# Layer 0's softmax division, taken apart into steps that lie in the next half head

## The chip, the cores and the metric

The kernel runs on one core of a Trainium2 chip. The metric is the device time of one execution in microseconds (us). Every time below comes from runs and from one profiled execution of the kernel before the change. The engines are named as the profile names them: PE (TensorE, with its weight loads as PEld), DVE (VectorE), ACT (ScalarE), POOL (GpSimd) and SP (SyncE, which here only issues transfers).

## The reference

Four images of 32 x 32 pixels and 384 channels go through four layers, each `x = x + layer(group_norm(x))`. All data are 32-bit floats.

```python
# layer 0: deformable attention, 6 heads of 64 channels, n = 1024 pixels
q = x @ w_q + b_q
offset = tanh(gelu(layer_norm(grouped_conv3x3(q))) @ w_offp) * 16
pos = offset + ref
xs = bilinear_sample(x, pos)                  # per group
k, v = xs @ w_k + b_k, xs @ w_v + b_v
attn = einsum('bmhc,bnhc->bhmn', q, k) * scale
bias = bilinear_sample(rpe, (ref - pos) / 2)  # 1024 x 1024 per head
attn = softmax(attn + bias, axis=-1)
out = einsum('bhmn,bnhc->bmhc', attn, v) @ w_out + b_out
# layer 1: attention of 12 heads of 32 channels, weighted by products of
#          sigmoid similarities, normalised over the queries
# layer 2: windowed sums of squares, num / denum
# layer 3: a 3 x 3 neighbourhood attention (softmax over 9), folded back
```

The change concerns the last step of layer 0's softmax: the division of `exp(...) @ v` by the sum of the exponentials.

## The kernel before, in words

Two generators write the program. `Front.layer0` is layer 0 of an image, `Trunk.image` is layers 1 to 3 of an image. Layer 0 of image 0 is written first, alone. Then the trunk of image b is written step by step, and after each step `Net.layer3` (the driver below) takes steps of layer 0 of image b + 1, as many as their yielded weights ask for. The trunk of the last image stands alone again. A scheduler then orders the instructions of each engine by dependence, priority and expected times; an instruction given to `keep_in_program_order` (`pin`) stays behind the one that was written before it on its engine. [...]

Layer 0's attention runs over six heads h and two halves q of 512 queries: twelve half heads an image, each one call of `head0(h, q)`. The keys j come in eight blocks of 128. For each j, POOL gathers a window of the position bias (`win`, L734), ACT and DVE interpolate it (`z`: L746, L747; `lg`: L751, L752), PE multiplies keys by queries (L755), DVE adds the product to the bias (L756) and keeps a running maximum (L759, L761). After the eighth block PE transposes the maxima (L768), DVE reduces them (`top`, L772), POOL makes a diagonal of them (L774), PE spreads it over the partitions (L776) and ACT copies it out (`tb`, L780). Then for each j DVE subtracts `tb` (L787), ACT takes the exponential (L788), and PE multiplies it by the values and by ones (L790), which gives the undivided output and the sums in one bank. ACT copies the output over the queries in `qpad` (L794) and the row of sums out (L797), and SP stores the row to `den` in DRAM (L798). Thirteen buffers hold the `lg` tiles: eight logits of the half head at work, the rest for the next one's bias, which the scheduler brings forward.

After two heads, `over_sums(k)` divides channel block k of `qpad` by the sums of heads 2k and 2k + 1. It loads the sums from DRAM with the pixels on the partitions (`dens`, two transfers, L807), takes the reciprocal (L808), stores it to `rden` (two transfers, L811), loads it back spread over 64 partitions per head into two `lg` tiles (four transfers, L816), and multiplies (two instructions, L821). After the third division, layer 0's output projection (L376, called from the loop at L427) reads `qpad`, DVE adds bias and residual (L432), and SP stores the result for the trunk.

In the trunk, layer 1 runs over six pairs of heads. The lines that matter here: Ln of the softmax sums (L1057) and the row of them stored and loaded again (L1063, L1011), four sigmoids of the similarities (L1081, after the matmuls L1074), logits (L1154) and their exponentials (L1162), the weights (L1184) and their product with the exponentials (L1193), and beside these the sums of the next pair (L1035, L1043, L1044). The other transfers of a pair are qa and ka (L1005), xg and gc (L1020, L1021), the values vp (L1102) and the result yd (L1215, from ACT's copy L1212). Exp, Sigmoid, Ln and Sqrt each make ACT load another table when they follow one another. Layer 2 ends with matmuls L1301, reciprocals L1323 and two more DVE steps (L1324, L1325), and statistics (L306, L307) for the norm of layer 3 (L330, L340), which needs its own weights `gmat`.

Of the kernel before, what the change touches and what calls it, by code (L numbers as in the profile page):

```python
# [21 lines left out]
ALU = mybir.AluOpType  # L22
# [4 lines left out]
P = 128  # L27
NB, HW, C = 4, 32, 384
N = HW * HW
KC = C // P  # L30
NJ = N // P
G, GC = 6, 64
# [32 lines left out]
def bc(ap, axis, n):  # L65

    u = ap.unsqueeze(axis)
    shape = list(u.shape)
    shape[axis] = n
    return u.broadcast_to(shape)  # L70


class Net:
# [183 lines left out]
    def layer0(self, b):  # L257

        if b == 0:
            for _ in self.front.layer0(b):  # L260
                pass
            self.done = self.ahead = 0.0
            self.fronts = (w for i in range(1, NB) for w in self.front.layer0(i))
# [135 lines left out]
class Front(Lane):  # L399


    def layer0(self, b):
        nc, v = self.nc, self.nc.vector
        with self.scope("l0"):
            self.qpad = self.wt([P, KC, PW, PW], "qpad")
            nc.gpsimd.memset(self.qpad, 0.0)

            self.kz = [self.wt([P, N], f"kz{r}") for r in range(2)]
            for r in range(2):
                nc.gpsimd.memset(self.kz[r][GC * (1 - r) : GC * (2 - r), :], 0.0)  # L410
            self.va = self.wt([P, NJ, C], "va")
            self.f = self.wt([P, 2, 2, NJ * G], "bias_f")
            self.widx = self.wt([P, 2, NJ * G], "widx", 1, I32)
            with self.scope("l0a"):
                yield from self.inputs0(b)
            with self.scope("l0b"):
                self.load_keys(0)
                for h in range(G):
                    if h + 1 < G:
                        self.load_keys(h + 1)  # L420
                    for q in range(2):
                        yield from self.head0(h, q)
                    if h % 2:
                        yield from self.over_sums(h // 2)
            with self.scope("l0c"):
                w = self.weights("w_out")
                for ko in range(KC):  # L427
                    rows = slice(ko * P, (ko + 1) * P)
                    x = self.wt([P, N], "res", 2)
                    nc.sync.dma_start(x, self.x0[b % 2][rows, :])  # L430
                    ps = self.dense_t(w, self.qpad, ko)
                    v.scalar_tensor_tensor(x, ps, self.col(C_BOUT, ko), x, ALU.add, ALU.add)  # L432
                    nc.sync.dma_start(self.x1[b % 2][rows, :], x)
                    yield 6
# [281 lines left out]
        rows = slice((h % 2) * GC, (h % 2 + 1) * GC)  # L716
        self.nc.sync.dma_start(self.kz[h % 2][rows, :], self.k0[h * GC : (h + 1) * GC, :])

    def head0(self, h, q):

        nc, v = self.nc, self.nc.vector
        f, kz, va = self.f, self.kz[h % 2], self.va
        k, r0 = h // 2, (h % 2) * GC
        rows = slice(r0, r0 + GC)
        other = slice(GC - r0, 2 * GC - r0)
        HH, HN = HW // 2, N // 2
        both = self.qpad[:, k, 1 + HH * q : 1 + HH * (q + 1), 1 : 1 + HW]
        queries = both[rows]
        logits = []
        rmax = self.wt([P, HN], "rmax", 2)  # L730
        for j in range(NJ):
            c = j * G + h
            win = self.wt([P, (HH + 1) * WROW], "win", 4)
            nc.gpsimd.indirect_dma_start(  # L734
                out=win,
                out_offset=None,
                in_=self.strips[:, :],
                in_offset=bass.IndirectOffsetOnAxis(
                    ap=self.widx[:, q, c : c + 1], axis=0
                ),  # L740
            )
            wv = win.rearrange("p (r c) -> p r c", c=WROW)
            sc = lambda i, t: f[:, i, t, c : c + 1]

            z = self.wt([P, HH, HW + 1], "z", 3)
            nc.scalar.activation(z, wv[:, 0:HH, 0 : HW + 1], AF.Copy, scale=sc(1, 1))  # L746
            v.scalar_tensor_tensor(  # L747
                z, wv[:, 1 : HH + 1, 0 : HW + 1], sc(0, 1), z, ALU.mult, ALU.add
            )
            lg = self.wt([P, HH, HW], "lg", 13)  # L750
            nc.scalar.activation(lg, z[:, :, 0:HW], AF.Copy, scale=sc(1, 0))  # L751
            v.scalar_tensor_tensor(lg, z[:, :, 1 : HW + 1], sc(0, 0), lg, ALU.mult, ALU.add)  # L752
            lf = lg.rearrange("p y x -> p (y x)")
            ps = self.bank()
            nc.tensor.matmul(ps, kz[:, j * P : (j + 1) * P], both, start=True, stop=True)  # L755
            v.tensor_tensor(lf, ps, lf, ALU.add)  # L756
            logits.append(lf)
            if j == 1:
                v.tensor_tensor(rmax, logits[0], lf, ALU.max)  # L759
            elif j > 1:  # L760
                v.tensor_tensor(rmax, rmax, lf, ALU.max)  # L761
            yield 3


        NI = HN // P
        ps = self.bank()
        for i in range(NI):
            nc.tensor.transpose(  # L768
                ps[:, i * P : (i + 1) * P], rmax[:, i * P : (i + 1) * P], self.ident
            )  # L770
        top = self.wt([P, NI], "top", 2)
        v.tensor_reduce(top, ps.rearrange("p (i n) -> p i n", i=NI), AX.X, ALU.max)  # L772
        diag = self.wt([P, NI, P], "diag", 1)
        nc.gpsimd.tensor_tensor(diag, bc(self.ident, 1, NI), bc(top, 2, P), ALU.mult)  # L774
        ps = self.bank()
        nc.tensor.matmul(  # L776
            ps, self.ones, diag.rearrange("p i n -> p (i n)"), start=True, stop=True
        )
        tb = self.wt([P, HN], "tb", 2)
        nc.scalar.copy(tb, ps)  # L780
        yield 3


        po = self.bank()
        for j in range(NJ):
            lf = logits[j]
            v.tensor_tensor(lf, lf, tb, ALU.subtract)  # L787
            nc.scalar.activation(lf, lf, AF.Exp)  # L788
            for out, w in ((rows, va[:, j, h * GC : (h + 1) * GC]), (other, self.ones[:, 0:GC])):
                nc.tensor.matmul(po[out, :], w, lf, start=j == 0, stop=j == NJ - 1)  # L790
            if j % 2:
                yield 2

        nc.scalar.copy(queries, po[rows, :].rearrange("p (y x) -> p y x", y=HH))  # L794
        o0 = other.start
        den = logits[0][o0 : o0 + 1, :]
        nc.scalar.copy(den, po[o0 : o0 + 1, :])  # L797
        nc.sync.dma_start(self.den[h][:, q * HN : (q + 1) * HN], den)  # L798
        yield 3

    def over_sums(self, k):

        nc, v = self.nc, self.nc.vector
        t = self.wt([P, 2, NJ], "dens", 2)
        for r in range(2):
            h = 2 * k + r
            nc.sync.dma_start(t[:, r, :], self.den[h].rearrange("o (p i) -> (o p) i", p=P))  # L807
        v.reciprocal(t, t)  # L808
        for r in range(2):
            h = 2 * k + r  # L810
            nc.sync.dma_start(self.rden[h].rearrange("o (p i) -> (o p) i", p=P), t[:, r, :])  # L811
        HH, HN = HW // 2, N // 2
        for q in range(2):
            inv = self.wt([P, HH, HW], "lg", 13)
            for r in range(2):
                nc.sync.dma_start(  # L816
                    inv[r * GC : (r + 1) * GC].rearrange("p y x -> p (y x)"),
                    self.rden[2 * k + r][0, q * HN : (q + 1) * HN].partition_broadcast(GC),
                )
            out = self.qpad[:, k, 1 + HH * q : 1 + HH * (q + 1), 1 : 1 + HW]  # L820
            v.tensor_tensor(out, out, inv, ALU.mult)  # L821
        yield 2


class Trunk(Lane):
# [717 lines left out]
```

## Time and profile before

| What | us |
|---|---|
| Median of 3 runs | 4879.74 |
| Lowest and highest of them | 4869.65, 4883.42 |
| The profiled execution | 4916.4 |
| Its span, first to last instruction | 4914.6 |

| Engine | busy us | share of the span |
|---|---|---|
| PE | 4251.9 | 87% |
| PEld | 1829.4 | 37% |
| DVE | 3177.4 | 65% |
| ACT | 2331.1 | 47% |
| POOL | 934.4 | 19% |

The shares are averages over stages with different limits. Layer 0 of image 0 takes about the first 650 us, and PE is busy in less than three quarters of most of it. Then PE is busy nine tenths of nearly every fortieth of the span, until layers 2 and 3 of the last image. The trunk of the last image starts near 4056 us. Stages are therefore read one by one, from windows of the trace. In the timeline lines of this document the first column is the start in us from the span's start and the second the length; in brackets stand the idle time of the engine ahead of the instruction and what ended it.

### The profile page before, as it was taken

The page shows a single profiled execution, that of the slowest core. Times are in us where ns is not written, and L with a number is a line of the kernel's source. Part 1 is how long each engine was busy: PE and PEld are TensorE (multiplying, and loading weights), DVE is VectorE, ACT ScalarE, POOL GpSimd, SP SyncE. Part 2 cuts the span into 40 slices and gives each one's busy share as a digit, 9 for nine tenths or more (in the row PEclk, how much of TensorE's full clock was granted, in tenths as well). Part 3 has the DMA queues.
Part 4 walks back from the last instruction along what each step waited for, and adds up shares of the span by engine and source line. Part 5 has one row for each costly group of instructions (what it writes and reads, how often), then busy time and mean ns, then how long its engine had stood idle before and what let it go on. Part 6 is the DMA issues. An engine that isn't in the chain of part 4 may idle for free.

```text
span 4914.6 us, 46753 instructions
## 1 busy us (share of the span) xinstructions
PE 4251.9 (87%) x15800; PEld 1829.4 (37%) x15800; DVE 3177.4 (65%) x5715; ACT 2331.1 (47%) x3623; POOL 934.4 (19%) x946
## 2 busy tenths in 40 slices
PE   5466677999999989889999989899999998999998
PEld 2222243333333453333333444343333335343444
DVE  3478827676878736577877763767687873455544
ACT  2155523565766213376666412356576721466630
POOL 1533203211212101331221110422121200000000
PEclk7677787999999989799999989799999998899998
DMA  5322244211212143331221123422121213201011
GB/s 116 106 81 87 69 128 143 92 55 38 76 47 74 33 145 111 104 95 49 66 58 58 55 75 111 151 88 58 32 78 44 78 34 111 91 24 30 18 38 39
DMA packets 230929, 366.84 MB, mean 75 GB/s; under 512 B 117476, under 2 KB 164673, under 8 KB 230689
## 3 DMA queue, kind: packets, MB, share of 16 engines
q1 hardware_dynamic: 169672, 197.36, 13.5%
q0 software_dynamic: 39936, 145.53, 9.7%
q10 hardware_dynamic: 21080, 20.96, 1.7%
q8 instruction: 125, 2.05, 0.2%
q14 instruction: 116, 0.94, 0.1%
HBM read 285.84 MB, written 78.21 MB: 74 GB/s over the span
## 4 chain that ended last, share of the span: by engine, by line
PE 50%; DVE 11%; ACT 11%; issue 5%; DMA 2%; POOL 1%; another core or an unknown queue 0%; SPq 0%; ACTq 0%; DVEq 0%; POOLq 0%
PE bank L1184 10%; PE big L376 5%; PE big L1154 5%; PE big L1035 4%; PE bank L755 4%; PE bank L790 4%; PE bank L390 3%; PE bank L1128 3%; ACT big L1044 3%; PE bank L1179 2%; PE big L1284 2%; DVE e L1193 2%; DVE nmax L1043 2%; ACT e L1162 1%; PE big L584 1%
## 5 line engine op out<-in xcount | busy, mean ns | idle before, releaser
L1193 DVE SCALAR_TENSOR_TENSOR e<-bank,gam,e 128x512 f32<-128x512 f32 x768 | 558.2, 749 | 568.3 <-ACT gn L1192 274.5
L1184 PE MATMUL bank<-sim,sg 128*128 128x512 f32 (+3 forms) x2304 | 879.6, 516 | 6.2 <-POOL sg L1139 3.7
L1044 ACT ACTIVATE big<-big,nmax 128x1024 f32<-128x1024 f32 x384 | 418.5, 1090 | 392.2 <-DVE nmax L1043 340.4
L734 POOL DMA_INDIRECT win<-strips,widx x384 | 421.2, 1097 | 876.6 <-DVE z L747 450.7
L1184 PEld LDWEIGHTS bank<-sim,sg 128*128 128x128 f32 x2304 | 408.7, 200 | 386.2 <-issue 303.6
L1162 ACT ACTIVATE e<-big 128x1024 f32<-128x1024 f32 x384 | 376.7, 1019 | 359.9 <-PE big L1154 354.7
L1043 DVE TENSOR_REDUCE nmax<-big 128x1 f32<-128x1024 f32 x384 | 453.7, 1219 | 74.4 <-PE big L1035 46.5
L1035 PE MATMUL big<-k,q 32*128 32x512 f32 x1536 | 353.6, 691 | 86.6 <-ACT e L1162 36.6
L1154 PE MATMUL big<-qa,ka 64*128 64x512 f32 x1536 | 412.9, 629 | 14.8 <-ACT big L1044 8.9
L1139 POOL TENSOR_SCALAR sg<-sim,gam 128x512 f32<-128x512 f32 x192 | 148.2, 774 | 1429.3 <-PE bank L1184 1135.5
L790 PE MATMUL bank<-lg,va 128*64 128x512 f32 x768 | 373.6, 635 | 39.8 <-ACT lg L788 39.7
L755 PE MATMUL bank<-qpad,kz 128*128 128x512 f32 x768 | 378.2, 622 | 21.4 <-DVE e L1193 13.2
L790 PE MATMUL bank<-lg,ones 128*64 128x512 f32 x768 | 372.9, 635 | 0.0
L746 ACT ACTIVATE z<-win,bias_f 128x528 f32<-128x528 f32 x384 | 277.2, 738 | 181.5 <-DVE lg L752 105.3
L752 DVE SCALAR_TENSOR_TENSOR lg<-z,bias_f,lg 128x512 f32<-128x512 f32 x384 | 300.8, 798 | 45.5 <-ACT lg L751 43.7
L747 DVE SCALAR_TENSOR_TENSOR z<-win,bias_f,z 128x528 f32<-128x528 f32 x384 | 292.0, 781 | 36.0 <-DMA win<-strips,widx 24.3
L652 POOL DMA_INDIRECT gat<-pairs,sidx x192 | 206.2, 1074 | 485.6 <-DVE ix_gt L464 241.6
L756 DVE TENSOR_TENSOR lg<-bank,lg 128x512 f32<-128x512 f32 x384 | 256.9, 685 | 60.3 <-PE bank L755 58.7
L787 DVE TENSOR_TENSOR lg<-lg,tb 128x512 f32<-128x512 f32 x384 | 250.6, 711 | 61.3 <-ACT tb L780 61.3
L751 ACT ACTIVATE lg<-z,bias_f 128x512 f32<-128x512 f32 x384 | 268.0, 719 | 44.3 <-DVE z L747 27.4
L788 ACT ACTIVATE lg<-lg 128x512 f32<-128x512 f32 x384 | 223.2, 630 | 85.4 <-DVE lg L787 85.1
L1154 PEld LDWEIGHTS big<-qa,ka 64*128 64x128 f32 x1536 | 135.8, 189 | 272.2 <-issue 157.0
(253 smaller groups left out, 5844.8 us busy)
## 6 DMA issues: line engine op xcount, KB each, us to landing
pairs<-xn SPq DMA_DIRECT2D x64, 192.0 KB
q<-qd SPq DMA_DIRECT2D x48, 256.0 KB
w<-in_gmat SPq DMA_DIRECT2D x16, 576.0 KB
w<-in_w_off SPq DMA_DIRECT2D x12, 576.0 KB
w<-in_Wqkv SPq DMA_DIRECT2D x12, 576.0 KB
a<-in_x SPq DMA_DIRECT2D x16, 384.0 KB
x<-a ACTq DMA_DIRECT2D x4, 1536.0 KB
k<-a SPq DMA_DIRECT2D x12, 512.0 KB
```

The source lines that it names most:

```text
L734: nc.gpsimd.indirect_dma_start(out=win, out_offset=None, in_=self.strips[:, :], in_offset=bass.IndirectOffsetOnAxis(ap=self.widx[:, q, c : ...
L747: v.scalar_tensor_tensor(z, wv[:, 1 : HH + 1, 0 : HW + 1], sc(0, 1), z, ALU.mult, ALU.add)
L752: v.scalar_tensor_tensor(lg, z[:, :, 1 : HW + 1], sc(0, 0), lg, ALU.mult, ALU.add)
L755: nc.tensor.matmul(ps, kz[:, j * P : (j + 1) * P], both, start=True, stop=True)
L790: nc.tensor.matmul(po[out, :], w, lf, start=j == 0, stop=j == NJ - 1)
L1035: nc.tensor.matmul(ps[r][:, h * 512 : (h + 1) * 512], self.q4[rows, i * P : (i + 1) * P], self.k4[rows, 0:512], start=True, stop=True,)
L1043: v.tensor_reduce(nmax[:, r, i : i + 1], ps[r], AX.X, ALU.max, negate=True)
L1044: nc.scalar.activation(ps[r], ps[r], AF.Exp, bias=nmax[:, r, i : i + 1], accum_out=den[:, r, i : i + 1],)
L1154: nc.tensor.matmul(ps[:, r, :], ka[rows, j * P : (j + 1) * P], qa[rows, cols], start=True, stop=True,)
L1162: nc.scalar.activation(e, ps, AF.Exp)
L1184: nc.tensor.matmul(ps[:, (mid - i0) * P :], sg[:, r, m, :], sim[:, r, m, mid * P : i1 * P], start=m == 0, stop=m == 1,)
L1193: v.scalar_tensor_tensor(e[:, r, :], ps, self.gam[:, 1:2], e[:, r, :], ALU.add, ALU.mult, accum_out=tot[:, r, h : h + 1],)
```

## The change

`over_sums` now issues only the two loads of `dens` at once and returns a generator of three steps: the reciprocal and the two `rden` stores; the four loads of the spread reciprocals; the two multiplies. `head0` takes this generator as `late` and advances it at three places of the next half head: after block j = 5 of the logits, and after blocks j = 0 and j = 5 of the exponentials. The reciprocal and the multiplies are pinned. After the last half head of an image the three steps follow one another as before. The weights yielded for an image's three divisions fall from 6 to 4, out of some 714.

```diff
@@ Front.layer0
+                late = iter(())
                 for h in range(G):
                     if h + 1 < G:
                         self.load_keys(h + 1)
                     for q in range(2):
-                        yield from self.head0(h, q)
+                        yield from self.head0(h, q, late)
                     if h % 2:
-                        yield from self.over_sums(h // 2)
+                        late = self.over_sums(h // 2)
+                for _ in late:
+                    yield 2
@@ Front.head0
+            if j == 5:
+                next(late, None)
             yield 3
...
                 nc.tensor.matmul(po[out, :], w, lf, start=j == 0, stop=j == NJ - 1)
+            if j in (0, 5):
+                next(late, None)
             if j % 2:
                 yield 2
@@ Front.over_sums
         for r in range(2):
             h = 2 * k + r
             nc.sync.dma_start(t[:, r, :], self.den[h].rearrange("o (p i) -> (o p) i", p=P))
-        v.reciprocal(t, t)
-        for r in range(2):
-            h = 2 * k + r
-            nc.sync.dma_start(self.rden[h].rearrange("o (p i) -> (o p) i", p=P), t[:, r, :])
-        HH, HN = HW // 2, N // 2
-        for q in range(2):
-            inv = self.wt([P, HH, HW], "lg", 13)
+        def rest():
+            pin(v.reciprocal(t, t))
             for r in range(2):
+                h = 2 * k + r
                 nc.sync.dma_start(
-                    inv[r * GC : (r + 1) * GC].rearrange("p y x -> p (y x)"),
-                    self.rden[2 * k + r][0, q * HN : (q + 1) * HN].partition_broadcast(GC),
+                    self.rden[h].rearrange("o (p i) -> (o p) i", p=P), t[:, r, :]
                 )
-            out = self.qpad[:, k, 1 + HH * q : 1 + HH * (q + 1), 1 : 1 + HW]
-            v.tensor_tensor(out, out, inv, ALU.mult)
-        yield 2
+            yield
+            HH, HN = HW // 2, N // 2
+            invs = []
+            for q in range(2):
+                inv = self.wt([P, HH, HW], "lg", 13)
+                for r in range(2):
+                    nc.sync.dma_start(
+                        inv[r * GC : (r + 1) * GC].rearrange("p y x -> p (y x)"),
+                        self.rden[2 * k + r][0, q * HN : (q + 1) * HN].partition_broadcast(GC),
+                    )
+                invs.append(inv)
+            yield
+            for q in range(2):
+                out = self.qpad[:, k, 1 + HH * q : 1 + HH * (q + 1), 1 : 1 + HW]
+                pin(v.tensor_tensor(out, out, invs[q], ALU.mult))
+
+        return rest()
```

More of the change, by code (lines that the diff above doesn't have):

```diff
@@ L717, in load_keys, with head0 @@
         self.nc.sync.dma_start(self.kz[h % 2][rows, :], self.k0[h * GC : (h + 1) * GC, :])
-    def head0(self, h, q):
+    def head0(self, h, q, late):
         nc, v = self.nc, self.nc.vector
@@ L801, in over_sums @@
     def over_sums(self, k):
-        nc, v = self.nc, self.nc.vector
+        nc, v, pin = self.nc, self.nc.vector, self.tc.keep_in_program_order
         t = self.wt([P, 2, NJ], "dens", 2)
```

## The prediction

> **What bounds the kernel now.** I read the windows of engine time by stage first. The first image's layer 0 stands alone; from L772 (one per half head) its half heads run so (each engine's busy us and count, then the PE clock, DMA share, GB/s):
>
> ```profile
> core 0: us, PE busy (x) PEld busy (x) DVE busy (x) ACT busy (x) POOL busy (x), PEclk, DMA share, GB/s
> 341.50:385.60 44.10, 24.62 (x58) 8.58 (x58) 26.64 (x43) 18.93 (x29) 8.19 (x7) 0.73 0.18 55
> 385.60:414.20 28.60, 18.82 (x54) 6.45 (x54) 27.19 (x42) 17.07 (x29) 9.94 (x10) 0.80 0.37 109
> 414.20:443.70 29.50, 20.29 (x54) 6.99 (x54) 26.49 (x41) 16.68 (x28) 9.92 (x9) 0.73 0.28 85
> 443.70:471.80 28.10, 18.85 (x55) 6.49 (x54) 25.94 (x40) 14.79 (x25) 12.45 (x10) 0.80 0.33 100
> 471.80:515.80 44.00, 23.88 (x58) 8.24 (x58) 26.69 (x43) 18.98 (x29) 9.18 (x8) 0.73 0.21 62
> ```
>
> An ordinary half head is DVE-bound: 26 to 27 of 28 to 29.5 us. The two that hold a division do the same DVE work in 44 us. The DVE timeline at the first of them says why (start, us, instruction, and in brackets the idle time before it):
>
> ```profile
> 360.92 0.25 DVE L808 RECIPROCAL dens<-dens 128x16 f32<-128x16 f32 x1 [9.87 <-DMA dens<-den]
> 361.09 1.32 DVE L752 SCALAR_TENSOR_TENSOR lg<-z,bias_f,lg 128x512 f32<-128x512 f32 x2
> 366.04 0.69 DVE L821 TENSOR_TENSOR qpad<-qpad,lg 128x512 f32<-128x512 f32 x1 [3.64 <-DMA lg<-rden]
> ```
>
> SP's queue in the same stretch, where issues stand by start and length:
>
> ```profile
> 359.25 0.35 SPq L807 DMA_DIRECT2D dens<-den  x1
> 361.19 0.81 SPq L811 DMA_DIRECT2D rden<-dens  x2
> 362.61 2.37 SPq L816 DMA_DIRECT2D lg<-rden  x4
> ```
>
> And the table of DVE's waits over the whole run (us in total, times, longest):
>
> ```profile
> DVE dens L808 <- DMA dens<-den: 28.9, 3, 9.9
> ```
>
> DVE reaches the reciprocal at 351.05 (360.92 - 9.87), while PE finishes the last L790 only at 356.8; the copy of the sums and two transfers follow. DVE, in order, stands until then, and again at L821. The waits of 28.9 us are three: the first image's. In images 1 to 3 layer 0 is woven into the trunk (layers 1 to 3 of the image before); there DVE finds L808 ready (0.1 us idle at most), and PE bounds. Two pairs of layer 1:
>
> ```profile
> 1240.80:1371.30 130.50, 118.87 (x471) 47.11 (x472) 112.53 (x204) 95.33 (x151) 37.75 (x37) 0.97 0.28 84
> 1371.30:1491.80 120.50, 115.51 (x468) 46.01 (x467) 85.64 (x169) 75.01 (x117) 14.11 (x16) 0.97 0.14 41
> ```
>
> PE is busy 91 and 96% of them. So the change can win only in the first image, and lose in the other three by what it does to the interleaving.
>
> **What the Trainium skill says.** "DMA: Bandwidth & Descriptors", Anatomy of one DMA, puts a fixed cost of about 2.0 us on a transfer, and says that a semaphore wait happens on the issuing sequencer, not in the DMA engines. The trace agrees roughly: the small dens load issued at 359.25 released DVE at 360.92 (1.7 us), and 366.04 is 2.2 us after the second lg issue ended. Hence a transfer queued behind a waiting one on SP is late too. "ScalarE: Activation LUTs", What ACT_TABLE_LOAD costs, gives about 1283 ns for a table load whatever the set; here all 142 took 1283 ns.
>
> **The change part by part**, from the two programs' instruction orders.
>
> *1. Image 0, divisions of heads 0/1 and 2/3.* Both dens loads stay where they are. The reciprocal moves behind most of the next half head's maxima, the multiplies behind six of its eight L787. After the last L787, DVE now has seven L747/L752 (4 x 0.77 + 3 x 0.75 = 5.3 us), which fill the 5.7 us until PE ends at 356.8, then L756 and L761, over 10 us. So dens (landed at 361) is there when the reciprocal comes, about 368; rden and lg follow by 375, the multiplies about 380. The divisor's half head should then last an ordinary 28.9 us (mean of 28.6, 29.5, 28.1, 29.3, 29.0, the last two being the half heads from 515.8 and 545.1) plus the division's own DVE work, 0.25 + 2 x 0.69 = 1.6. Gain: 2 x (44.05 - 28.9 - 1.6) = **27.1 us**. The direct stalls, 9.87 + 3.64 + 9.26 + 3.66 = 26.4, agree. Lower end 16.5: the seven fillers bring nothing (2 x 5.3 off). Upper end 34: the holes ahead of L787 in these half heads (3.9 and 4.3 us on ACT's tb, unfilled before, filled now) come on top.
>
> *2. Image 0, heads 4/5.* No half head follows; reciprocal and multiplies keep their places on DVE, with waits of 9.8 and 5.7 us. Gain 0; nothing excludes 1 us either way.
>
> *3. The wait that is moved.* SP's two rden stores (0.81 us) now wait for the later reciprocal. In image 0 only the next den store and a key load are behind them, not due yet. In images 1 to 3, layer 1's loads are: qa/ka, the lse store and row, yd. The reciprocal stands about 6 us after a pair's Ln; the lse store went out at 9.1 to 10.4. Once the lse row is also behind the first yd store, at about 12.2 instead of 10.5; it lands by 14.5 and PE asks for it (L1154) at 18.5. Cost 0, covered by the sims. For one division of images 1 and 2 the fourth lg load is behind the xg loads (18.1 to 19.5), lands near 23.3, and the multiply comes near 23: 0 to 1 us on DVE, with L1193 next at 27. Cost 0. POOL issues nothing of the division; its gathers move with their L746/L747.
>
> *4. Table loads, images 1 to 3.* Before, in two of five shared pairs the first L788 Exps come between the four L1081 sigmoids; afterwards in all five. ACT gets 142 + 18 = 160 table loads. Bounds: 0 (covered) to 18 x 1.283 = 23.1 us. The trace has both patterns: in the first 40 us after Ln, PE is idle 4.7 and 5.0 us in the split pairs, 6.2, 3.5 and 4.2 in the other three. Turning those into 4.85 costs -1.35 + 1.35 + 0.65 = 0.65 us an image, **2 us**. L1154 even starts sooner (18.5 against 19.3 to 21.6).
>
> *5. Spread of bias work.* L747s per pair went 16, 6, 26, 6; now 16, 11, 21, 11. PE's idle beyond the first 40 us was 5.7, 1.8, 5.4, 1.5: what counts is whether a pair has much. The pairs with 11 are between; I take 2.5 each, 0.85 more: +1.7 an image, **5 us**; ends 0 and 3 x 7.5 = 23.
>
> *6. Layer 2 to 3, images 1 to 3.* Before, 4 of layer 2's last L1301 ran ahead of 16 of 18 L376; now 12 L376, which need the last multiplies, run first, and the gmat load for the layer 3 norm (before at 1723.7; PE waited 4.7 us for it) is mostly behind two result stores. Against that only 6 L376, not 16, stand between the sums and the norm. From L772 (1684.5) to the norm's L340 (1747.1) DVE has some 50 us of work in 62.6, 12.6 idle; my walk through the new order gives 9 to 17. Taken as 0; ends -10 and +15 in all.
>
> Sum: -27.1 + 2 + 5 = -20. The profiled execution took 4916.4 us (span 4914.6 and 1.8 around it): 4896 for its like. It is 0.75% above the median 4879.74, and no step grows with that, so **4860 us**.
>
> **Rivals.**
> - *The interleaving takes back the gain.* The table loads are exposed (23) or the bias work bunches (23): -27 + 23 is about 4876. For it: sigmoids release PE (L1074, L1154), and a load more between them is on that chain. Against it: point 4's split pairs.
> - *The stall only changes its name.* In image 0 the next half head's L755 cannot start before PE's L790 ends (5.7 us after the last L787), and DVE waits at L756 instead. Gain 16.5 less 7: 4870. Against it: ordinary half heads have that boundary and last 28.9.
> - *The change does not do what it says*, the reciprocal still standing ahead of its data: 4880. The instruction order speaks against it.
> - *Slower: layer 2's end hangs on the division.* In PE's order the last L1301 of layer 2 is behind 12 L376 waiting for the last multiplies. If the chain is serial there, each of images 1 to 3 pays 12 L376 (5.6 us at 0.47), the gmat load from issue to landing (4.5), the unfilled tb hole ahead of L787 (3.8), and, where the next image's transposes and statistics come ahead of the norm, as in image 2, some 5 more: 14 to 19 each, say 45 in all: 4880 - 27 + 45 = 4898. It decides from 42/3 = 14 us each. Against it: DVE's reciprocals (L1323, 6.55 us each) now stand before, so the multiplies' data are there, and before already had waits of that size.
>
> **How the numbers follow.** A measurement of this kernel tells about 0.3% from no change, 14.6 us: faster is below 4865, slower above 4894. First theory, 4860, own range 4845 to 4867: 0.60, nearly all of it faster. Interleaving takes it back: 0.17, same. Stall renamed: 0.08, a quarter of it faster. No effect: 0.05. Slower rival: 0.10, nine tenths of it above 4894. Together: faster 0.60, same 0.31, slower 0.09. The range, 4842 to 4881, leaves out the slower rival and a tail below.
>
> **What would show it.** Right: in the first image's layer 0 all middle half heads near 29 us and the division's near 30.5; idle before the reciprocal there for the last division alone (about 10 us); PE busy in pairs still 91 to 96%; 160 table loads. Wrong: DVE idle before L756 or L787 in those half heads above 5 us (stall renamed); pairs of images 1 to 3 summing to over 10 us more an image (interleaving); PE or DVE idle over 25 us between the last L772 and the layer 3 norm (slower rival). A gain over 40 us would mean that the trunk was waiting for layer 0 somewhere that I do not see.

## The result, and the profile after

| Kernel | median us | lowest to highest | ratio to before [95%] |
|---|---|---|---|
| before (4 runs beside it) | 4881.58 | 4869.65 to 4886.24 | 1 |
| after (4 runs) | 4913.03 | 4905.38 to 4918.05 | 1.0067 [1.0044, 1.0089] |

The change makes the kernel 0.67% slower, some 32 us, where 20 us of gain were predicted. The profiled execution of after took 4905.38 us, its span is 4903.6. That is below the span of before in the prediction (4914.6), although after is the slower kernel by its medians: single profiles differ by that much. The accounts below therefore use kernels profiled on one chip, and say so where they cannot.

The lines of after stand about 19 numbers further down than those of before: the reciprocal is L819 (was L808), its stores L822 (L811), the spread loads L831 (L816), the multiplies L839 (L821), `top` L778 (L772), the subtraction of `tb` L793 (L787), `exp @ v` L796 (L790), layer 2's matmuls L1320 (L1301), its steps on DVE L1334, L1336, L1342 to L1344 (L1315, L1317, L1323 to L1325), the residual L435 (L432).

**Layer 0 of the first image did what was predicted.** These are the windows of its half heads, from one L778 to the next, with the columns of the prediction's first windows:

```profile
core 0: us, PE busy (x) PEld busy (x) DVE busy (x) ACT busy (x) POOL busy (x), PEclk, DMA share, GB/s
341.70:371.30 29.60, 20.27 (x54) 6.98 (x54) 25.50 (x41) 16.26 (x27) 15.16 (x10) 0.73 0.35 98
371.30:402.80 31.50, 20.91 (x58) 7.53 (x58) 28.93 (x45) 16.92 (x28) 9.49 (x8) 0.77 0.29 84
402.80:433.20 30.40, 20.20 (x54) 6.99 (x54) 27.47 (x43) 18.02 (x29) 10.64 (x10) 0.72 0.32 93
433.20:461.50 28.30, 19.16 (x54) 6.77 (x54) 26.35 (x41) 16.73 (x28) 10.34 (x10) 0.80 0.34 99
461.50:490.70 29.20, 20.33 (x54) 6.99 (x54) 24.91 (x40) 15.61 (x26) 11.04 (x10) 0.73 0.35 100
```

The 44.1 and the 44.0 us are gone: 29.6 and 29.2, and the two half heads that took over the multiplies last 31.5 each. The DVE timeline of after at the first division shows how. In before the reciprocal and the multiply each had idle time ahead of them (9.87 and 3.64 us). DVE did no later work meanwhile: ACT had finished the first L751 at 358.7, and the first L752 began at 361.09, behind the reciprocal. Now neither the reciprocal nor the multiply has a bracket:

```profile
367.28 0.68 DVE L765 TENSOR_TENSOR rmax<-rmax,lg 128x512 f32<-128x512 f32 x1
367.88 0.24 DVE L819 RECIPROCAL dens<-dens 128x16 f32<-128x16 f32 x1
376.31 3.70 DVE L793 TENSOR_TENSOR lg<-lg,tb 128x512 f32<-128x512 f32 x6 [0.89 <-ACT tb L786]
379.94 1.28 DVE L839 TENSOR_TENSOR qpad<-qpad,lg 128x512 f32<-128x512 f32 x2
```

SP's queue in after, same place: the load of the sums goes out at 362.0, six microseconds before the reciprocal wants it, and the spread loads are out by 372.0 for a multiply at 379.9.

```profile
362.03 0.35 SPq L816 DMA_DIRECT2D dens<-den  x1
368.15 0.81 SPq L822 DMA_DIRECT2D rden<-dens  x2
369.61 2.37 SPq L831 DMA_DIRECT2D lg<-rden  x4
```

And from DVE's table of waits in after, from 233 to 650 us (in total, times, longest): of the three waits of 28.9 us one is left, that of the last division, as predicted.

```profile
DVE dens L819 <- DMA dens<-den: 9.9, 1, 9.9
```

The loss lies elsewhere, and exceeds the gain.

### The profile page after: what moved, and what is told of

Read it like the earlier page. It is cut to its first block, busy times and chain, and to the rows that moved or that the text cites. A ratio compares the mean times of both kernels' runs of the same rounds, so it can differ in the third digit from the quotient of the medians.

```text
span 4903.6 us, 46825 instructions
## 1 busy us (share of the span) xinstructions
PE 4239.5 (86%) x15800; PEld 1815.2 (37%) x15800; DVE 3171.7 (65%) x5715; ACT 2354.4 (48%) x3641; POOL 950.1 (19%) x946
## 4 chain that ended last, share of the span: by engine, by line
PE 34%; DVE 10%; ACT 8%; issue 2%; DMA 2%; POOL 1%; SPq 0%; ACTq 0%; DVEq 0%; POOLq 0%
PE bank L1203 7%; PE big L1173 3%; PE big L376 3%; PE big L1054 3%; PE bank L759 2%; PE bank L390 2%; PE bank L796 2%; ACT big L1063 2%; PE bank L1147 2%; DVE nmax L1062 2%; PE bank L1198 2%; PE big L1303 2%; DVE e L1212 1%; DVE dn L1342 1%; ACT e L1181 1%
## 5 line engine op out<-in xcount | busy, mean ns | idle before, releaser
L1203 PE MATMUL bank<-sim,sg 128*128 128x512 f32 (+3 forms) x2304 | 860.5, 506 | 2.6 <-DVE e L1212 2.6
L1203 PEld LDWEIGHTS bank<-sim,sg 128*128 128x128 f32 x2304 | 398.2, 196 | 373.8 <-issue 290.6
L796 PE MATMUL bank<-lg,va 128*64 128x512 f32 x768 | 382.8, 643 | 50.1 <-ACT lg L794 49.9
L796 PE MATMUL bank<-lg,ones 128*64 128x512 f32 x768 | 382.6, 643 | 0.0
L756 DVE SCALAR_TENSOR_TENSOR lg<-z,bias_f,lg 128x512 f32<-128x512 f32 x384 | 290.4, 769 | 57.6 <-ACT lg L755 55.5
L751 DVE SCALAR_TENSOR_TENSOR z<-win,bias_f,z 128x528 f32<-128x528 f32 x384 | 291.2, 780 | 36.0 <-ACT z L750 35.2
L793 DVE TENSOR_TENSOR lg<-lg,tb 128x512 f32<-128x512 f32 x384 | 246.7, 706 | 92.8 <-ACT tb L786 92.7
L759 PEld LDWEIGHTS bank<-qpad,kz 128*128 128x128 f32 x768 | 135.5, 192 | 265.0 <-issue 116.0
```

What stands on the lines that cost most here:

```text
L751: v.scalar_tensor_tensor(z, wv[:, 1 : HH + 1, 0 : HW + 1], sc(0, 1), z, ALU.mult, ALU.add)
L1203: nc.tensor.matmul(ps[:, (mid - i0) * P :], sg[:, r, m, :], sim[:, r, m, mid * P : i1 * P], start=m == 0, stop=m == 1,)
```

## The experiments

**Where: runs that split the images (one chip).** The first four ran on one chip, where before took 4908.7 us. `b` is the image; `over_sums_at_once` is before's `over_sums`.

*e1_before_again*: before, unchanged, for a trace on this chip.

> The kernel before, unchanged, for a trace and times on the chip of the runs that follow. Both theories: within 0.3% of the kernel before. If its profiled span is near 4880 and not 4914.6, the first trace of before was a slow-clocked one, and every stage of it has to be read again here.

*e2_img0_only*: the late steps in image 0 alone.

```diff
-                    if h % 2:
+                    if h % 2 and b == 0:
                         late = self.over_sums(h // 2)
+                    elif h % 2:
+                        yield from self.over_sums_at_once(h // 2)
```

> The late steps in image 0 alone; images 1 to 3 divide at once, with the instruction order of the kernel before. Theory A (the gain in image 0 stands and images 1 to 3 lose more than it by their new order): 4880 - 25 = 4855, ratio 0.995. Theory B (the time won in image 0 is given back through a lower granted PE clock later on): 4875 to 4885, ratio 1.000, with image 0's layer 0 shorter by 20 us or more and a lower clock in images 1 to 3.

*e3_img123_only*: the same with `b > 0`.

> The late steps in images 1 to 3 alone; image 0 divides at once, as in the kernel before. Theory A: images 1 to 3 lose 55 us by their order, so 4880 + 55 = 4935, ratio 1.011. Theory B: the loss is that of the whole change, 4913, ratio 1.007.

*e4_after_again*: after, unchanged.

> The changed kernel again on the same chip: 4913 by both theories, ratio 1.0067; its trace against that of the kernel before on the same chip should show where images 1 to 3 lose: theory A expects it in the stretches from layer 2 to the end of layer 3 and in the split pairs, at an equal clock.

Measured: e1 0.9994 [0.9981, 1.0008]; e2 0.9966 [0.9952, 0.9981]; e3 1.0085 [1.0052, 1.0118]; e4 1.0071 [1.0044, 1.0099]. Image 0 gains, images 1 to 3 lose more. Theory B, that a lower granted clock takes back the gain of image 0, fails on e2: it keeps the gain, at a mean clock of 0.909 against 0.905 in e1's profile. The interval of e3 alone would have allowed both theories. The stages, read off the traces in us (an "end" runs from the last `top` of the image whose layer 0 closes there to the first Ln of the next image's layer 1; the third runs to the end of the span):

| Kernel | layer 0 of image 0, to its last top | to the first Ln | layer 1's six pairs, from first Ln to last top, three images | end 1 | end 2 | end 3 | span |
|---|---|---|---|---|---|---|---|
| e1 (before) | 603.3 | 249.0 | 2505.0 | 325.9 | 333.5 | 901.5 | 4918.2 |
| e2 (image 0 only) | 577.7 | 241.6 | 2505.7 | 319.3 | 328.8 | 904.6 | 4877.7 |
| e3 (images 1 to 3) | 603.0 | 247.7 | 2500.5 | 327.3 | 358.3 | 919.2 | 4956.0 |
| e4 (after) | 577.3 | 241.3 | 2497.8 | 334.5 | 362.9 | 921.6 | 4935.4 |

Each row is one execution; those of e1 and e3 were 10 and 6 us slower than the median of their kernel, that of e2 7 us faster, that of e4 was the median. Image 0 gives 25.6 and 26.0 us (e2 and e4 against e1). The pairs do not grow: 2500.5 and 2497.8 against 2505.0. The ends of images 2 and 3 do: in e3 by 24.8 and 17.7 us, in e4 by 29.4 and 20.1. (Of e4's 8.6 in end 1 little is the change's: e3 has 1.4 there, and e2, in which images 1 to 3 are untouched, differs from e1 by 6.6.)

These lengths need care, because the last `top` that parts a pair from an end belongs to layer 0, and it moves against the trunk. The count behind "PE busy" in the windows of the pairs of image 2 shows it, first in e1, then in e4:

```profile
2010.80:2848.70 837.90, 782.79 (x2940) 318.26 (x2941) 612.43 (x1150) 499.82 (x770) 163.32 (x165) 0.95 0.22 62
1985.40:2827.20 841.80, 774.39 (x2922) 307.30 (x2923) 608.61 (x1149) 508.26 (x775) 165.50 (x165) 0.96 0.22 62
```

| Kernel | matmul records in the pairs of images 1, 2, 3 | us from the first Ln of layer 1 to that of the next image: 1, 2, 3 |
|---|---|---|
| e1 (before) | 2940, 2940, 2940 | 1158.4, 1171.4, 1079.1 |
| e2 (image 0 only) | 2940, 2940, 2940 | 1155.1, 1163.2, 1083.5 |
| e3 (images 1 to 3) | 2936, 2922, 2920 | 1163.3, 1198.9, 1085.5 |
| e4 (after) | 2936, 2922, 2920 | 1166.7, 1204.7, 1087.5 |

With the change the last `top` comes earlier against the trunk, by 18 and 20 records in images 2 and 3, and that work of the trunk falls into the end instead. The last column runs between two marks of the trunk and is free of this. By it image 2 loses 27.5 and 33.3 us (e3 and e4), image 1 4.9 and 8.3, image 3 6.4 and 8.4; e2, whose images 1 to 3 are unchanged, differs from e1 by -3.3, -8.2 and 4.4. So image 2 carries most of the loss, and what images 1 and 3 lose is hardly more than two executions differ. Nor are the pairs of image 2 free: PE is idle for 67.4 us of them in e4, for 55.1 in e1 (length less busy time in the two lines).

**What happens in those ends.** Windows from the last `top` to the third residual sum of the output projection, for images 1, 2 and 3. Before again, then after again:

```profile
1684.90:1743.30 58.40, 49.22 (x127) 19.71 (x126) 48.90 (x38) 9.21 (x13) 11.71 (x6) 0.97 0.20 65
2848.70:2907.90 59.20, 49.93 (x134) 20.42 (x132) 48.89 (x38) 9.21 (x13) 12.36 (x7) 0.97 0.20 61
4016.70:4076.60 59.90, 50.64 (x127) 20.30 (x126) 48.95 (x39) 9.21 (x13) 11.70 (x6) 0.94 0.20 63
```

```profile
1650.80:1710.70 59.90, 50.60 (x127) 19.70 (x126) 48.01 (x39) 9.42 (x14) 11.01 (x5) 0.97 0.19 63
2827.20:2901.80 74.60, 60.48 (x140) 23.88 (x139) 47.07 (x38) 8.31 (x13) 10.49 (x5) 0.91 0.15 49
4013.80:4089.60 75.80, 61.80 (x145) 24.44 (x143) 47.07 (x38) 8.34 (x13) 10.50 (x5) 0.91 0.16 50
```

In images 2 and 3 DVE has no more work than before (47.1 against 48.9 us), but 15 to 16 us more of time: it is idle. PE has some 11 us more to do there (60.5 and 61.8 against 49.9 and 50.6): the matmuls of the trunk that in before ran ahead of the last `top`. Image 1, with the same source, is nearly untouched. The wait table of DVE in after again, in the second of these windows (total, times, longest), names the holes:

```profile
DVE none L1334 <- PE big L1320: 9.5, 1, 9.5
DVE res L435 <- PE big L376: 7.2, 2, 5.1
DVE qpad L839 <- DMA lg<-rden: 4.4, 2, 3.9
```

The timelines tell the order behind them. DVE in before again, image 2: the eight L787 of the last half head lie between layer 2's steps, the reciprocal of the sums stands ahead of layer 2's last long reciprocal (L1323), and while that runs the spread reciprocals come; the multiply waits for nothing.

```profile
2850.40 1.23 DVE L1315 TENSOR_SCALAR none<-big 128x1024 f32<-128x1024 f32 x1 [1.03 <-PE big L1301]
2866.06 4.38 DVE L787 TENSOR_TENSOR lg<-lg,tb 128x512 f32<-128x512 f32 x5
2882.07 0.20 DVE L808 RECIPROCAL dens<-dens 128x16 f32<-128x16 f32 x1
2883.28 6.55 DVE L1323 RECIPROCAL dn<-dn 128x1024 f32<-128x1024 f32 x1
2890.88 0.68 DVE L821 TENSOR_TENSOR qpad<-qpad,lg 128x512 f32<-128x512 f32 x1
```

DVE in after again, image 2: all eight L793 come first, then DVE stands for layer 2's first result, then runs layer 2's three long reciprocals, and the division's pinned reciprocal is behind them. Nothing is left to cover its transfers.

```profile
2830.92 4.91 DVE L793 TENSOR_TENSOR lg<-lg,tb 128x512 f32<-128x512 f32 x8 [3.02 <-ACT tb L786]
2845.31 1.23 DVE L1334 TENSOR_SCALAR none<-big 128x1024 f32<-128x1024 f32 x1 [9.48 <-PE big L1320]
2877.40 0.20 DVE L819 RECIPROCAL dens<-dens 128x16 f32<-128x16 f32 x1
2882.91 0.69 DVE L839 TENSOR_TENSOR qpad<-qpad,lg 128x512 f32<-128x512 f32 x1 [3.93 <-DMA lg<-rden]
2889.82 1.28 DVE L435 SCALAR_TENSOR_TENSOR res<-big,cols,res 128x1024 f32<-128x1024 f32 x1 [5.06 <-PE big L376]
```

SP had issued the load of those sums long before, 33 us ahead of the reciprocal (2844.06):

```profile
2844.06 0.34 SPq L816 DMA_DIRECT2D dens<-den  x1
2877.63 0.81 SPq L822 DMA_DIRECT2D rden<-dens  x2
```

And PE in after again, where the projection's matmuls stand for the multiply and layer 2's last four are behind them (the profile records each of these matmuls twice). The third line is the next image's transposes:

```profile
2883.66 9.51 PE L376 MATMUL big<-qpad,w 128*128 128x512 f32 x16 [5.05 <-DVE qpad L839]
2893.01 3.60 PE L1320 MATMUL big<-s,w 128*128 128x512 f32 x8
2911.02 5.11 PE L533 MATMUL bank<-ident,a 128*128 128x128 f32 x24 [9.25 <-DMA a<-in_x]
```

Layer 2's last step (L1344) starts at 2898 there, 70.8 us after the `top`; in before again it is 44.8. Layer 3 and layer 0 of the next image then start late. Their normalised inputs, `xh` for layer 3 and `a` for the next image (L357), come this long after the `top`:

| Kernel | image 1: xh, a | image 2: xh, a | image 3: xh |
|---|---|---|---|
| e1 (before) | 62.8, 85.8 | 63.6, 86.5 | 65.3 |
| e4 (after) | 65.4, 87.4 | 107.8, 105.6 | 81.9 |

In image 2 the next image's transposes, for which PE waits 9.25 us until their loads land, have also come ahead of layer 3's norm; in before again they are behind it. Counted from the first Ln instead of the moved `top`, the later of the two inputs is 25 us late in image 2 (949.6 us against 924.4), and the only one in image 3 just 6 (905.6 against 899.8).

**Why images 2 and 3 have another order than 1: the count of steps.** The source is the same for the three, so something adds up from image to image. The driver counts a layer 0 as 714 steps (`FRONT_STEPS`); with the yielded weights down from 6 to 4, a layer 0 of after has 712. Each image's layer 0 thus runs two steps further ahead of the trunk than the one before it, in keeping with the falling counts of records above. (After the last half head the three steps do not quite follow one another as before, either: at the two stops between them the driver writes steps of the trunk.) The theory: that drift tips the scheduler's order. Its rivals: the pins, or the place of the late steps.

*e5_yields_only*: before, with only the yields as in after (none after two divisions, 4 after the third).

```diff
-        yield 2
+        if k == G // 2 - 1:
+            yield 4
```

> The kernel before with only the yields of its divisions changed: none after heads 1 and 3, 4 after head 5; each division still at once and unpinned. Theory P (phase: the missing yields shift layer 0 against the trunk, so that at the end of layer 2 the last half head's exponentials come ahead of layer 2's own steps): slower by 25 to 45 us, ratio 1.005 to 1.009, with the stretch from the last top (L772) to the residual sums (L432) of images 2 and 3 longer by 10 us or more each. Theory N (the pins: the last reciprocal is held behind layer 2's steps on DVE): no change, ratio 0.999 to 1.001.

*e6_no_pins*: after, without its pins.

```diff
-            pin(v.reciprocal(t, t))
+            v.reciprocal(t, t)
...
-                pin(v.tensor_tensor(out, out, invs[q], ALU.mult))
+                v.tensor_tensor(out, out, invs[q], ALU.mult)
```

> The whole change without its three pins. Theory P: as slow as the changed kernel or 10 us less, ratio 1.004 to 1.007. Theory N: images 1 to 3 lose nothing, image 0 keeps its gain: ratio 0.995 to 0.997.

*e7_keep_yields*: after, with before's `yield 2` after heads 1, 3 and 5 (sum 6), the last division's steps at once and pinned.

```diff
+                        if h + 1 == G:
+                            for _ in late:
+                                pass
+                        yield 2
-                for _ in late:
-                    yield 2
```

> The whole change with the yields of before: 2 after each of heads 1, 3 and 5, and the last division's steps drained at once; the pins stay. Theory P: images 1 to 3 lose nothing in the stretches from layer 2 to layer 3, image 0 keeps its gain: ratio 0.994 to 0.997. Theory N: as slow as the changed kernel, ratio 1.005 to 1.008.

*e8_last_at_once_yields*: late steps after heads 1 and 3 only; the last division as in before, not pinned; sum 6.

```diff
-                    if h % 2:
+                    if h % 2 and h + 1 < G:
                         late = self.over_sums(h // 2)
-                for _ in late:
-                    yield 2
+                        yield 2
+                    elif h % 2:
+                        yield from self.over_sums_at_once(h // 2)
```

> The late steps after heads 1 and 3 alone, in all images; the last division at once and unpinned, and the yields of before, so that the order from layer 2 to layer 3 is that of before. Both theories: ratio 0.994 to 0.997, as with image 0 alone. If it is slower than image 0 alone by over 10 us, the late steps cost something inside the pairs of images 1 to 3, which neither theory has.

Measured side by side (before 4910.29 us): e5 1.0126 [1.01, 1.0152], e6 1.0128 [1.0103, 1.0153], e7 0.9965 [0.994, 0.999], e8 0.9925 [0.9903, 0.9947]. Both kernels that keep the sum at 6 win; both with 4 lose, one of them without any late step. Theory P, of the count, had every sign right but not every size: e5 and e6 lose more than it gave, e8 gains more. The pins are not the cause of the loss: without them it is larger. The windows of e5 as above (last `top` to third residual sum, images 2 and 3) show the late end although nothing is pinned, but half of it, 66 to 67 us against the 75 of after (e6, also without pins, has 65.9 and 68.8):

```profile
2874.10:2940.30 66.20, 58.06 (x140) 23.04 (x138) 48.22 (x39) 8.31 (x13) 10.54 (x5) 0.95 0.17 57
4061.50:4128.90 67.40, 59.04 (x145) 23.57 (x144) 48.22 (x38) 8.34 (x13) 10.47 (x5) 0.95 0.17 56
```

So the tipped order lengthens this place by some 7 us in e5. The further 7 to 9 us of after fit the pin on the last reciprocal, since e6, with after's counts of records but no pins, does not have them; a kernel without that one pin alone was not run. e7 teaches what to look at: there the third residual sum comes 68.2, 70.7 and 73.9 us after the `top`, later than in before in every image, but `xh` at 50.7, 53.3 and 53.3, earlier by 10 to 12, and `a` (images 1 and 2) 9 to 11 later; its ends take 325.4, 342.1 and 901.4 us, beside 325.9, 333.5 and 901.5 in e1 (on another chip). A late residual alone is therefore not the price. What fits the table of `xh` and `a` is that the price is paid where both inputs are late, as in image 2 of after; that was not tried by itself.

e5 and e6 lose inside the pairs too. e6's traces show one place: the unpinned reciprocal floats ahead of the trunk's work and DVE stands for its data.

```profile
1189.26 0.25 DVE L819 RECIPROCAL dens<-dens 128x16 f32<-128x16 f32 x1 [3.44 <-DMA dens<-den]
```

e6's pairs take 2557.4 us from first Ln to last `top`, against 2497.8 of e4 on another chip. The waits of its reciprocals there sum to 10.1 us (3.4, 3.4, 2.1 and 1.1), so they are a small part of these 60 us; the rest stays open.

**The count alone.** Two runs bring the sum and what the driver counts together again, leaving everything else of after, and another takes before out of step without touching layer 0.

*e9_sum6*: after, the two stops of the last division yield 3 each (sum 6).

```diff
                 for _ in late:
-                    yield 2
+                    yield 3
```

> The whole change, but 3 instead of 2 yielded at each of the two stops of the last drain: 6 an image, as before. The order at the end of layer 2 is then in all three images that of image 1 in the changed kernel, and ACT still has 160 table loads. Theory D (the missing 2 of 714 steps an image add up, and from image 2 on tip the end of layer 2 into the slow order): the stretch from the last top (L772) to the residual sums (L432) is 58 to 63 us in all three images, not 75 in two; ratio 0.994 to 0.998. Rival T (the table loads and the late steps within the pairs are what costs): ratio 1.004 or more.

*e10_fs712*: after, the driver counts 712.

```diff
-TRUNK_STEPS, FRONT_STEPS, LEAD = 1109.0, 714.0, 0.1
+TRUNK_STEPS, FRONT_STEPS, LEAD = 1109.0, 712.0, 0.1
```

> The whole change with the interleaver's constant FRONT_STEPS at 712, the number of steps an image's layer 0 now has. 136 table loads; the order at the end of layer 2 is the same in all images, but another one than before. Theory D: no drift, so images 2 and 3 lose no more than image 1; ratio 0.993 to 1.000. If it is above 1.004, keeping the sum is not what matters, but the order that happens to come out.

*e11_last_at_once_again*: e8 once more, beside these.

> The late steps after heads 1 and 3 alone with the yields of before, a second time, beside the two others on this chip: ratio 0.990 to 0.996.

*e12_before_fs716*: before, the driver counts 716.

```diff
-TRUNK_STEPS, FRONT_STEPS, LEAD = 1109.0, 714.0, 0.1
+TRUNK_STEPS, FRONT_STEPS, LEAD = 1109.0, 716.0, 0.1
```

> The kernel before, with one number changed: the driver counts 716 steps for a layer 0 that yields 714, so each layer 0 is two steps further on against the trunk, as in the kernel after, but no late step, no pin and no other place of a yield. Theory (the missing two steps alone tip the order at the end of layer 2): from the last top to the third residual sum 65 to 68 us in images 2 and 3 against 59 to 60, 58 to 60 in image 1; in image 2 the next image's transposes ahead of the norm again, 10 to 15 us more; in all 20 to 35 us slower, ratio 1.004 to 1.007. If the pairs lose as they did with the yields moved to the last division (17 us an image), up to 1.013. Rival (the tipped order needs the late steps or the pins): 0.999 to 1.001, and 58 to 61 us in all three.

Measured: e9 0.9961 [0.9947, 0.9976], e10 0.993 [0.9902, 0.9957], e11 0.9954 [0.9931, 0.9976] (before 4881.56 us); e12 1.0137 [1.0113, 1.016] (before 4917.2 us). With the sum at 6 the same windows of e9 are back at 58, and `xh` comes at 63.7, 63.6 and 63.8 us:

```profile
1658.00:1716.10 58.10, 50.83 (x130) 20.20 (x128) 47.85 (x38) 9.43 (x14) 12.14 (x6) 0.94 0.20 64
2814.90:2873.40 58.50, 51.35 (x133) 20.59 (x132) 47.90 (x39) 9.40 (x14) 12.47 (x7) 0.94 0.19 63
3968.90:4027.30 58.40, 51.11 (x132) 20.52 (x130) 47.84 (x38) 9.38 (x14) 12.16 (x6) 0.94 0.19 63
```

One number in the driver also spoils before: e12 shows the late end in images 1 and 3 (image 2's third residual is nearly in time, yet its `xh` comes at 94.3 us, behind the next image's norm, as in after). It had been expected in images 2 and 3.

```profile
1696.20:1763.30 67.10, 55.04 (x130) 21.39 (x128) 49.10 (x38) 9.79 (x14) 10.89 (x5) 0.90 0.19 56
2888.10:2949.70 61.60, 51.52 (x126) 19.68 (x125) 49.30 (x38) 8.32 (x13) 10.87 (x5) 0.92 0.19 61
4071.80:4138.00 66.20, 58.32 (x144) 23.35 (x142) 46.99 (x38) 8.32 (x13) 10.49 (x5) 0.95 0.18 57
```

e12 lost more than the 20 to 35 us that the ends alone would give: from its first Ln to the last `top` the pairs took 2531.3 us over three images, 26 more than in e1, on another chip. So a drift of two steps an image is enough to make the kernel slower by 1% and more, with no late step at all. In after the pairs do not grow; e6, without pins, does not escape. That the pins are what protects the pairs fits e4 and e6 but was tried only in that one way.

The counts of the earlier table, for the other runs (chips differ):

| Kernel | steps counted less steps yielded | matmul records in the pairs of images 1, 2, 3 | us from first Ln to the next image's: 1, 2, 3 |
|---|---|---|---|
| e5 (yields only) | 2 | 2936, 2922, 2920 | 1183.5, 1182.7, 1097.2 |
| e6 (no pins) | 2 | 2936, 2922, 2920 | 1191.8, 1209.4, 1092.7 |
| e12 (before, 716) | 2 | 2936, 2936, 2919 | 1182.8, 1189.1, 1100.0 |
| e7 (yields of before) | 0 | 2940, 2940, 2940 | 1157.6, 1174.8, 1077.6 |
| e8, e11 (last at once) | 0 | 2940, 2940, 2940 | 1164.7, 1162.7, 1079.9 and 1146.5, 1153.8, 1075.9 |
| e9 (sum 6) | 0 | 2936, 2936, 2936 | 1156.8, 1157.2, 1083.1 |
| e10 (712) | 0 | 2936, 2936, 2936 | 1149.9, 1150.1, 1072.6 |

The yields alone (e5) give exactly the counts of after. Every kernel whose layer 0 yields what the driver counts is faster than before and keeps its records from image to image; every kernel that is off by two is slower and does not. How the scheduler turns the drift into the tipped order was not followed, and e12, late in image 1 already, shows that it need not build up as in after; a drift of another size or the other way was not tried.

e7 to e11 and e2 beat both kernels; most of their intervals overlap, and none of them can be called the best. Nor is all of their gain image 0's: the pairs of e10 take 2467.2 us, those of e9, measured beside it, 2515.9, with the same matmul records and some 177 us of idle PE in both. The matmuls themselves took less time in e10 (PE busy for 2290 us against 2338, at a granted clock of 0.97 against 0.95 to 0.96); why was not shown.

## Why the prediction was wrong, point by point

The predicted time was 4860, the measured one 4913, outside the range. The step that failed is term 6, the end of layer 2, taken as 0. What came true is nearest to the slower rival, to which the prediction gave one chance in ten, at 4898.

1. *Image 0, heads 0/1 and 2/3: right.* 27.1 us predicted; 25.6 and 26.0 measured at the last `top`, and by the mechanism described. (Its upper end of 34 is not the sum of its addends: 27.1 + 3.9 + 4.3 is 35.3.)
2. *Image 0, heads 4/5: right.* The wait of 9.9 us stays, and the multiply's: 5.5 us in after.
3. *The wait that is moved: not contradicted.* The pairs did not grow (e3 and e4 against e1), so nothing shows that the transfers behind the moved stores on SP were missed; what makes PE idle longer in image 2's pairs was not taken apart. The fixed 2.0 us that the prediction quotes from the Trainium skill ("DMA: Bandwidth & Descriptors", Anatomy of one DMA) are given there for transfers that GpSimd issues; these are issued by SP, and the trace's own 1.7 and 2.2 us are what holds for them.
4. *Table loads: right in number, and no price shows.* e9 has 39 sigmoid loads and 34 of the exponential, as after; before has 30 and 19:

```profile
L1100 ACT ACT_TABLE_LOAD x39 | 50.0, 1283 | 24.2 <-DMA lse<-lrow 15.3 <-PE big L1093 8.7
L794 ACT ACT_TABLE_LOAD x34 | 43.6, 1283 | 0.6
```

   Yet e9 (160 loads) is at 0.9961 and e2 (142 loads, late steps in image 0 alone) at 0.9966, and in one series of runs PE is idle for some 177 us of the pairs with 160 loads (e9), with 142 (e11) and with 136 (e10). The 1283 ns that the Trainium skill gives ("ScalarE: Activation LUTs", What ACT_TABLE_LOAD costs) hold for each; 18 more beside a busy PE cost nothing that shows. The same passage adds some 1380 ns of drain to every switch, which the prediction left out; 98 of the 160 loads in e4 have less than 0.1 us of idle ACT on either side, so no such time stands there.
5. *Spread of bias work: right within what can be read.* Points 4 and 5 together were to cost 7 us. First Ln to last `top` took 7.2 us less in e4 than in e1, but held 42 matmul records fewer, an estimated 11 us at the 0.27 us each of e1's line above; so some 4 us of cost are left, and the drift is in them too. Two pairs of after, beside image 1's layer 0, where PE is busy 91 and 94% of the time, against 91 and 96% in the two pairs of before:

```profile
1205.30:1338.10 132.80, 121.51 (x470) 46.91 (x469) 105.06 (x198) 93.48 (x145) 31.50 (x31) 0.95 0.26 73
1338.10:1463.70 125.60, 117.60 (x470) 45.81 (x469) 91.68 (x175) 80.96 (x126) 20.25 (x21) 0.97 0.17 50
```

6. *Layer 2 to 3, images 1 to 3: here it failed.* The prediction saw the order (the last L1301 behind L376 that need the multiplies) and set its cost to 0, with +15 as the upper end for all three images. Measured at the ends: 1.4, 24.8 and 17.7 us in e3, 43.9 in all; between marks of the trunk 4.9, 27.5 and 6.4, 38.8 in all. The term was argued from one walk through image 1, where the outcome is indeed small, and then taken for all three; images 2 and 3 have another order. The prediction's own sign of it stands in after: from the last `top` to the first L340 of a norm behind it DVE is idle for 41.3 and 28.2 us in images 2 and 3, over the 25 that it named, and for 12.0 in image 1. It set the slower rival aside because "DVE's reciprocals (L1323, 6.55 us each) now stand before, so the multiplies' data are there": in images 2 and 3 the division's own reciprocal stands behind them as well, so the data are not there (3.9 us at the multiply, 5.1 at the residual).

   The slower rival had this chain right, and in image 2 the next image's transposes ahead of the norm. Its price, "14 to 19 each, say 45 in all", came near the total by luck: image 2 pays most of it, images 1 and 3 little.

What the prediction left out is the cause of that order. The change's description gives the fall of the weights from 6 to 4; no part of the sum priced it. It looks like bookkeeping, and it is the part of the change that decides: with it 1.0071, without it 0.993 to 0.9961.

## What to carry to other kernels

When a step is moved in a program that interleaves two streams by counted steps, the count is part of the change: keep the sum, or tell the driver the new one, before judging the move. A drift of two in 714 showed nowhere near the edit, and in after it grew from one repetition to the next, so compare the order at the seams in every repetition, not in the first. Where a mark that divides two stages can itself move, measure between marks that do not. The pinned late instructions cost nothing visible where work followed them; at the end of a stage, where nothing was left to cover the transfers, the multiply stood 3.9 us and the residual 5.1.

## What the runs showed of the hardware

Before alone had medians of 4881.6, 4908.7, 4910.3, 4881.6 and 4917.2 us in five series of runs: 0.7% between them, as much as the whole effect. The argument therefore rests on ratios within one series and, for the first four experiments, on traces of one chip; where e5 to e12 are set against e1 or e4 the chips differ, and a difference of some microseconds says nothing. Stages of unchanged code moved by as much: from the last `top` of image 0 to the first Ln e8 took 249.6 us and e11, the same kernel, 239.8.
